# Reordering the start, the first block's close and the last block of a conditioned transformer block

## The chip, the cores and the metric

The kernel runs on one core of a Trainium2 chip. The metric is the device time of one execution in microseconds (us). A core has five engines with queues of their own: TensorE (PE) for matmuls, VectorE (DVE), ScalarE (ACT), GpSimd (POOL), and SyncE (SP), which here issues nearly all DMAs. Each engine works its queue in order; engines wait for each other through semaphores.

## What is computed

One transformer block with adaptive layer norm, for x of shape (8, 1024, 512) in float32, 16 heads of 32 columns, an MLP of 2048:

```python
mod = silu(condition) @ Wada + bada
sh_a, sc_a, gt_a, sh_m, sc_m, gt_m = split(mod, 6, axis=1)
xn = layernorm(x) * g1 + be1
xm = xn * (1 + sc_a) + sh_a
x = x + gt_a * attention(xm)          # causal; qkv = xm @ Wqkv, then @ Wproj + bproj
xn = layernorm(x) * g2 + be2
xm = xn * (1 + sc_m) + sh_m
x = x + gt_m * (gelu(xm @ W1 + b1) @ W2 + b2)
```

## The kernel before

The 8 sequences of 1024 tokens are cut into 16 blocks of 512 tokens, numbered 0 to 15. Even blocks are the first half of a sequence and attend to themselves; odd blocks attend to both halves. The 16 heads go in four groups of four (`g` 0 to 3).

The program is written out by Python in the order in which it is to run: what each engine does is fixed by the order of emission. Two streams are woven together by a planner that keeps its own estimate of each engine's time (`now`, `note`, `due`).

**The attention stream** (`attend`, line 1390). For each group of each block it sends *score tiles* (`scores`, L1206: up to 512 columns for four heads into the PSUM tile `st`; DVE adds the mask at L1218 and takes row maxima at L1226; `maxima_rows` brings the maxima to where they are subtracted, L1266) and *weight units* (`weights_T`, L1292 and L1303 into the same PSUM tile `st`; ACT takes the exponential at L1315; POOL clears the diagonal's upper half at L1320). A first-half block has 3 weight units per group and 3 score tiles, a second-half block 7 and 7. Weight units are the *slots* of the stream. In each slot the unit before is closed: `close` calls `weigh` (L1343, weights times values into `po`), POOL adds the weights up for the denominator (L1427), and after the last unit of a group `finish` sums over partitions by a matmul with ones (L1361), ACT copies (L1367, L1370), DVE inverts in four parts (L1376), and POOL writes the quotient over q (L1381). When group 3 of a block has its quotient, the block is "attended". After closing, a slot sends score tiles ahead for the next group, as far as `upto` says:

```python
                    upto = len(units)
                    if nxt < len(groups):
                        lo, m = first_unit[groups[nxt]], len(score_units(*groups[nxt]))
                        upto = lo + min(m, -(-(k + 2) * m // n_slots))
```

Group 3 of block 0 so has three score tiles of block 1 sent in its first slot, two in its second, and two more in its third, after two that were sent with group 2; and since a unit is closed in the slot after it, the last one of block 0 is closed after block 1's first weight unit.

**The linear stream** (`linear`, `perform`, line 1011) works through a list of steps per window, `plan` (line 228). Steps are: modulation columns (`mod`), gates, transposing and modulating normalized tokens (`at` for attention, `mt` for the MLP, both `modulated`, L622 and L593/L599), projections `k`, `q`, `v` (`strassen`: seven half-size products instead of eight, L199), the output projection with the residual (`proj`, `project_out`, which starts when its block is attended and ends with the second norm), up-projections `u` (four of them) and down-projections `d` (four parts, seven products in all). Some steps run as *side threads* beside the main list (`start`): `at`, `mt`, and the last two products of each `strassen`. `work` (line 1104) sends the next piece of the thread that waits least; at a tie, the side thread's. Attention waits (`step_aside`, L1133) let linear work in, and a pace (`stream`) keeps the two in step. For the values of block 15 attention stops until `v` of that block is done (`close`, line 1440).

The second norm has DVE statistics (L539), then two ACT steps, a root (L547) and the normalizing (L558). While both streams run, these two are *excursions*: `run_excursions(1)` lets one out per slot (line 1415).

**Weights** come through a ring of nine tiles of 256 KB in the order of the steps' pieces (`order`, `fetch`, L328 to L332, on SP); a tile is refilled when it is released. The seven products need sums of quarters of each weight. For the first use of k, q and v these sums are made on the core (`weight_sums`, L668, four DVE subtractions or additions of 128x512) and kept in DRAM (L659, on SP); those of the MLP are prepared along the way on DVE or POOL (`preparation`, `either`, L156 or L159).

**The start** (window -1). `at 0` transposes block 0 into the PSUM tile `early` (of four banks) without the gains, then waits for them:

```python
        if key == "a0":
            written["early"] = 0.0
            yield ["columns"], []
            for c in range(NC):
                modulate(c, early[:, c, :], "st")
```

and the second modulation waits for `early`, so its matmuls stand behind the sixteen transposes. **The end.** Window 15 has the MLP of block 13 to finish (`late`: three down parts), the projection of block 14, `v` of block 15 and most of block 14's MLP; window 16 has the last two down parts of block 14, and block 15's projection and MLP.

Of the kernel before, what the change touches and what calls it, by code (L numbers as in the profile page):

```python
# [22 lines left out]
def kernel(  # L23
# [36 lines left out]
    P = 128  # L60
# [164 lines left out]
    def mlp_steps(n):  # L225
        return [("u", n, i) for i in range(NQ)] + [("d", n, part) for part in range(4)]

    plan = {
        -1: [("at", 0), ("mod", 0), ("mod", 1), ("norm_columns_a",), ("load_xa", 1)]
        + [("k", 0), ("norm_a", 1), ("q", 0), ("at", 1), ("v", 0)],  # L230
        0: [("load_xa", 2), ("preps",), ("k", 1), ("norm_a", 2), ("gates", "a"), ("q", 1)]
# [3 lines left out]
    for w in range(1, NB):  # L235
        n = w - 1
        m = mlp_steps(n)
        even = blocks[n][1] == 0
        rows_a = [("rows", blocks[n][0], "a")] if even else []
        rows_m = [("rows", blocks[n][0], "m")] if even else []  # L240
        own = m[:1] + ([("load_xa", w + 2)] if w + 2 < NB else []) + m[1:3]
        own += [("norm_a", w + 2)] if w + 2 < NB else []
        if w == NB - 1:
            steps = late + [("load_xr", n)] + rows_a + [("proj", n), ("v", w)]
            steps += [("mt", n)] + rows_m + own + m[3:6]
            late = m[6:]
        else:

            steps = late + [("v", w), ("load_xr", n)] + rows_a + [("proj", n), ("k", w + 1)]
            if w == 1:  # L250
                steps = [("load_xr", n)] + rows_a + [("proj", n)]
            steps += [("mt", n), ("q", w + 1)] + rows_m + own
            at = [("at", w + 2)] if w + 2 < NB else []
            if blocks[w][1] == 0:

                steps += m[3:5]
                late = m[5:6] + at + m[6:]
            else:
                steps += m[3:6] + at
                late = m[6:]  # L260
        plan[w] = steps
    n = NB - 1
    plan[NB] = [("load_xr", n), late[0], ("proj", n), late[1], ("mt", n)] + mlp_steps(n)

# [20 lines left out]
    def pieces_of(step):  # L285

        kind = step[0]
        if kind == "mod":
            return [(Wada, step[1], kh, fh) for kh, fh in RAW]
        if kind == "gates":  # L290
            return [(Wada, GATES[step[1]][0], kh, fh) for kh, fh in RAW]
        if kind == "proj":
            return [(Wproj, 0, k) for k in range(NC)]
        if kind == "d":
            return [
                (W2, i, *AT[a]) if a in AT else (W2, i, a)
                for a in DOWN_ORDER[step[2]]
                for i in range(NQ)
            ]
        if raw_step(step):  # L300
            return [(*source_of(step), kh, fh) for kh, fh in RAW]
# [143 lines left out]
    columns_of = {}  # L445
    written["columns"] = written["early"] = NEVER
    gate_rows = {}
# [80 lines left out]
    def normalize(tiles, key, sources):  # L528
# [24 lines left out]
        def apply():  # L553
            for t, xt in enumerate(tiles):
                xh = xt
                if key[0] == "m":
                    xh = tmp.tile([P, D], F32, tag="hat", name=f"xh_{key}_{t}", bufs=NTT)
                nc.scalar.activation(  # L558
                    xh, xt, AF.Identity, bias=offset[:, t : t + 1], scale=rstd[:, t : t + 1]
                )  # L560
                note_act(800, None, [("rstd", key)], [("hat", key, t)])
                got.append(xh)
            hats[key] = got
# [3 lines left out]

    def modulated(key, b, guards):
        for t in ("B11", "B21", "B22", "T1", "T2", "T3", "T4"):
# [17 lines left out]
        at = {t: (key, t) for t in part}  # L587

        def modulate(c, place, source):
            gain, shift = columns_of[key[0]]  # L590
            writes = [at["B11"], at["T1"]] if c < 2 else [at["B21"], at["B22"]]
            if sooner([source], writes, 770, 780) == "DVE":
                nc.vector.tensor_scalar(  # L593
                    xm[:, c, :], place, gain[:, c, b : b + 1], shift[:, c, b : b + 1],
                    ALU.mult, ALU.add,
                )
                note("DVE", 770, [source], writes)
            else:
                nc.scalar.activation(  # L599
                    xm[:, c, :], place, AF.Identity,  # L600
                    bias=shift[:, c, b : b + 1], scale=gain[:, c, b : b + 1],
                )
                note_act(780, None, [source], writes)
# [4 lines left out]
        if key == "a0":  # L608

            early = ps_st.tile([P, NC, TB], F32, tag="st", name="early")  # L610
        for c in range(NC):
            if key != "a0":
                if c:
                    yield [("hat", key, 0)], [BANK]
                bank = lin_bank()
                place, source = banks[bank], ("l", bank)
            else:
                place, source = early[:, c, :], "st"
            for t in range(NTT):
                if t or c:  # L620
                    yield [("hat", key, t)], []
                nc.tensor.transpose(place[:, ts(t, P)], got[t][:, ts(c, P)], ident)  # L622
                note_pe(TR, "whole", [("hat", key, t)], [source])
            if key != "a0":
                modulate(c, place, source)
                live[bank] = False
        if key == "a0":
            written["early"] = 0.0
            yield ["columns"], []
            for c in range(NC):  # L630
                modulate(c, early[:, c, :], "st")
        nc.vector.tensor_tensor(part["T2"], part["B22"], part["T1"], ALU.subtract)  # L632
# [28 lines left out]
    def weight_sums(step, part):  # L661
# [4 lines left out]
        for j, (out, a, b, op) in enumerate(SUMS):  # L666
            got[out] = stage[:, j, :].rearrange("p (k n) -> p k n", n=HB)
            nc.vector.tensor_tensor(got[out], got[a], got[b], op)  # L668
            note("DVE", 700, [], [("sums", *step, out)], port=True)
            keep(w, i, out, stage[:, j, :])  # L670
# [26 lines left out]
    def run_preparation(everything=False):  # L697
        while prepared[0] is not None:
# [4 lines left out]
            try:  # L703
                prepared[0][1] = next(prepared[0][0])
            except StopIteration:
                prepared[0] = None

    tail_key = [None]

    def strassen(step, x, dest, target, row, done):  # L710
# [300 lines left out]
    def perform(step):  # L1011
# [3 lines left out]
        elif kind == "norm_columns_a":  # L1015
            columns_of["a"] = norm_columns("a", 0, 1, O_G1, O_BE1)
            written["columns"] = 0.0
        elif kind == "gates":
# [22 lines left out]
        elif kind == "at":  # L1041
            n = step[1]
            guards = [("m used", n - 3)] if n > 2 else [("v done", 0)] if n == 2 else []
            start(modulated(f"a{n}", blocks[n][0], guards))
        elif kind == "mt":
            n = step[1]
            guards = [("v done", n + 1)]
            start(modulated(f"m{n}", blocks[n][0], guards))
        elif kind == "k":
# [340 lines left out]
    def attend():  # L1390
        previous = None
        for n in range(NB):
# [19 lines left out]
            for g, k, upto in slots:  # L1412
# [9 lines left out]
                if k > 0:  # L1422
                    acc, first = totals[n, g]
                    for _, c0, w in parts:
                        for j in range(HPG):
                            into = acc[:, j, TB - w :]
                            nc.gpsimd.tensor_tensor(into, into, pT[:, j, c0 : c0 + w], ALU.add)  # L1427
# [113 lines left out]
```

## Time and profile before

| | us |
|---|---|
| median of 3 runs | 3687.08 (3687.07 to 3687.18) |
| profiled execution | 3685.5 |
| its span, first to last instruction | 3683.6 |
| PE busy | 3578.0 |
| DVE, POOL, ACT busy | 2158.7, 2030.0, 1330.8 |

The profile is of one execution. Its page gives busy time, the span in 40 slices (busy tenths) and the costliest groups; the trace behind it can be asked for busy time by stage, for waits and for a timeline. A wait is idle time of an engine ahead of an instruction, with the instruction or DMA that ended it. The granted clock of PE is 1.00 when it runs at full speed and 0.5 when at half; over the whole span it was 0.992. [...]

### The profile page before, as it was taken

The page shows a single profiled execution, that of the slowest core. Times are in us where ns is not written, and L with a number is a line of the kernel's source. Part 1 is how long each engine was busy: PE and PEld are TensorE (multiplying, and loading weights), DVE is VectorE, ACT ScalarE, POOL GpSimd, SP SyncE. Part 2 cuts the span into 40 slices and gives each one's busy share as a digit, 9 for nine tenths or more (in the row PEclk, how much of TensorE's full clock was granted, in tenths as well). Part 3 has the DMA queues.
Part 4 walks back from the last instruction along what each step waited for, and adds up shares of the span by engine and source line. Part 5 has one row for each costly group of instructions (what it writes and reads, how often), then busy time and mean ns, then how long its engine had stood idle before and what let it go on. Part 6 is the DMA issues. An engine that isn't in the chain of part 4 may idle for free.

```text
span 3683.6 us, 121126 instructions
## 1 busy us (share of the span) xinstructions
PE 3578.0 (97%) x54821; PEld 1770.6 (48%) x54821; DVE 2158.7 (59%) x2455; ACT 1330.8 (36%) x1415; POOL 2030.0 (55%) x2052
## 2 busy tenths in 40 slices
PE   7979999999999999999999999999999999998989
PEld 4424445445454455544545454454544445454445
DVE  5756676564755647465564656646666465664542
ACT  2324334252343523335242352424524244341421
POOL 1676745656456563556636665356653556445661
PEclk9989999999999999999999999999999999999999
DMA  5642333434334343433434333343333433334334
GB/s 182 202 135 90 109 106 105 127 102 130 102 114 119 108 123 110 131 95 107 125 107 139 96 96 119 111 133 102 102 119 111 136 105 108 107 106 123 90 110 133
DMA packets 307893, 430.34 MB, mean 117 GB/s; under 512 B 25900, under 2 KB 176236, under 8 KB 307380
## 3 DMA queue, kind: packets, MB, share of 16 engines
q1 hardware_dynamic: 307264, 422.56, 38.2%
q8 instruction: 432, 7.08, 0.8%
q14 instruction: 81, 0.66, 0.1%
q10 hardware_dynamic: 116, 0.03, 0.0%
HBM read 394.12 MB, written 28.38 MB: 115 GB/s over the span
## 4 chain that ended last, share of the span: by engine, by line
PE 86%; DVE 7%; ACT 2%; POOL 2%; issue 2%; DMA 0%; SPq 0%; ACTq 0%; POOLq 0%; DVEq 0%
PE bank L199 58%; PE st L1292 8%; PE sc L1206 8%; PE po L1343 7%; DVE mx L1226 2%; PE st L1303 2%; PE bank L1361 2%; POOL pT L1427 1%; PE bank L622 1%; ACT pT L1315 1%; DVE hT L928 1%; DVE sc L1218 1%; DVE xr L156 1%; DVE t_m L156 1%; PE bank L1266 0%
## 5 line engine op out<-in xcount | busy, mean ns | idle before, releaser
L1427 POOL TENSOR_TENSOR pT<-pT,pT 128x512 f32<-128x512 f32 (+3 forms) x1280 | 1209.0, 979 | 550.1 <-ACT pT L1315 383.8
L1315 ACT ACTIVATE pT<-st 128x2048 f32<-128x2048 f32 (+1 forms) x320 | 546.6, 1708 | 1019.4 <-PE st L1303 956.9
L199 PE MATMUL bank<-w,hT 128*32 128x256 f32 x14336 | 808.7, 380 | 5.0 <-DVE hT L928 2.2
L1226 DVE TENSOR_REDUCE mx<-sc 128x4 f32<-128x2048 f32 (+3 forms) x384 | 669.0, 1756 | 208.2 <-PE sc L1206 201.6
L199 PEld LDWEIGHTS bank<-w,hT 128*32 128x32 f32 x14336 | 453.2, 110 | 357.9 <-issue 61.3
L199 PE MATMUL bank<-xm_m,w 128*32 128x256 f32 x8192 | 506.4, 380 | 0.8 <-DVE u_u L191 0.8
L1320 POOL TENSOR_SCALAR_AFFINE_SELECT pT<-pT 128x512 f32<-128x512 f32 x256 | 178.1, 708 | 575.2 <-ACT pT L1315 574.9
L199 PE MATMUL bank<-t_m,w 128*32 128x256 f32 x6144 | 383.1, 380 | 2.4 <-DVE t_m L632 1.0
L1292 PE MATMUL st<-qT,kT 32*128 32x512 f32 (+3 forms) x3072 | 342.9, 530 | 35.9 <-DVE mx L1226 34.7
L199 PEld LDWEIGHTS bank<-xm_m,w 128*32 128x32 f32 x8192 | 254.3, 110 | 249.3 <-issue 95.8
L1206 PE MATMUL sc<-kT,qT 32*128 32x512 f32 (+3 forms) x3072 | 340.2, 527 | 12.6 <-DVE mx L1226 6.5
L1343 PE MATMUL po<-pT,v 128*32 128x512 f32 (+3 forms) x3072 | 315.1, 497 | 6.5 <-POOL pT L1320 6.5
L1218 DVE TENSOR_TENSOR sc<-sc,mask 128x512 f32<-128x512 f32 (+1 forms) x192 | 168.0, 875 | 249.4 <-PE sc L1206 221.6
L199 PEld LDWEIGHTS bank<-t_m,w 128*32 128x32 f32 x6144 | 193.0, 110 | 174.3 <-issue 50.2
L199 PE MATMUL bank<-w,qT 128*32 128x512 f32 x2048 | 241.5, 598 | 6.1 <-POOL qT L1381 3.2
L199 PE MATMUL bank<-xm_a,w 128*32 128x256 f32 x3968 | 244.2, 382 | 2.0 <-ACT xm_a L599 2.0
L1376 DVE RECIPROCAL rec<-rec 128x128 f32<-128x128 f32 x256 | 223.7, 918 | 21.6 <-ACT rec L1367 21.6
L1292 PEld LDWEIGHTS st<-qT,kT 32*128 32x128 f32 x3072 | 129.7, 185 | 201.9 <-issue 60.6
L1206 PEld LDWEIGHTS sc<-kT,qT 32*128 32x128 f32 x3072 | 126.7, 184 | 176.0 <-ACT pT L1315 84.7
L191 DVE TENSOR_TENSOR hT<-bank,u_u 128x512 f32<-128x512 f32 x192 | 130.4, 686 | 120.4 <-PE bank L199 118.4
L199 PE MATMUL bank<-t_a,w 128*32 128x256 f32 x2944 | 186.6, 382 | 0.0
L1315 ACT ACT_TABLE_LOAD x88 | 112.9, 1283 | 183.5 <-PE st L1303 182.8
(184 smaller groups left out, 3546.8 us busy)
## 6 DMA issues: line engine op xcount, KB each, us to landing
w<-in_L_cond_W_dram SPq DMA_DIRECT2D x384, 256.0 KB, 2.9
w<-kept_up_S SPq DMA_DIRECT2D x256, 256.0 KB, 2.6
w<-kept_down_S SPq DMA_DIRECT2D x256, 256.0 KB, 2.7
w<-kept_qkv_S SPq DMA_DIRECT2D x180, 256.0 KB, 2.9
w<-in_L_cond_Wqkv_dram SPq DMA_DIRECT2D x147, 256.0 KB, 3.5
hat<-in_x_dram SPq DMA_DIRECT2D x64, 256.0 KB, 3.4
w<-in_L_cond_Wproj_dram SPq DMA_DIRECT2D x64, 256.0 KB, 3.4
xr<-in_x_dram SPq DMA_DIRECT2D x64, 256.0 KB, 4.4
```

Of the source, the lines that this page charges most:

```text
L156: nc.vector.tensor_tensor(out, a, b, op)
L191: nc.vector.tensor_tensor(out, src, other, op)
L199: nc.tensor.matmul(ps[r, :], lhsT[:, r], rhs, start=start, stop=stop, skip_group_check=True)
L1206: nc.tensor.matmul(sc[:, j, c0 : c0 + w], qTs[n][r, g, ts(qt, P)], keys_of(n, kh)[r, g, :w], start=True, stop=True, skip_group_check=True,)
L1218: nc.vector.tensor_tensor(diagonal, diagonal, mask[:, :span].unsqueeze(1).to_broadcast([P, HPG, span]), ALU.add,)
L1226: nc.vector.tensor_reduce(mx[:, kh, qt, :], sc[:, :, c0 : c0 + w], axis=AX.X, op=ALU.max)
L1292: nc.tensor.matmul(st[:, j, c0 : c0 + w], kT[r, g, ts(k % NTT, P)], qT[r, g, TB - w :], start=(c0 == 0), stop=False, skip_group_check=True,)
L1315: nc.scalar.activation(pT[:, :, :used], st[:, :, :used], AF.Exp, scale=scale)
L1320: nc.gpsimd.affine_select(diagonal, diagonal, pattern=[[0, HPG], [1, P]], compare_op=ALU.is_ge, fill=0.0, base=0, channel_multiplier=-1,)
L1343: nc.tensor.matmul(po[r, TB - w :], v[:, k % NTT, g * P + j * hd : g * P + (j + 1) * hd], pT[:, j, c0 : c0 + w], start=(k == 0), stop=last ...
L1376: nc.vector.reciprocal(some, some)
L1427: nc.gpsimd.tensor_tensor(into, into, pT[:, j, c0 : c0 + w], ALU.add)
```

## The change

Three edits.

1. *Start.* In window -1 the modulations go first, then a new step `sums` for k, q and v each, well ahead of their projections; the sums are made on POOL instead of DVE. `at 0` follows the gains and goes through the three ordinary banks, as every other block's does. A one-column square root loads the ACT table early, and the normalizing of block 0 alternates between ACT and DVE.
2. *Block 0's last group.* Its first and second slots send no score tiles of block 1; in the third, one tile is sent, then the unit just made is closed at once (values, denominator, quotient), then the other six tiles follow.
3. *End.* In window 15 only the first of the three old down parts stays ahead of block 14's projection and `mt`; the other two follow, then `v`. In window 16 the last down part of block 14 runs as a side thread (`beside`) next to block 15's projection instead of behind it.

```diff
-        -1: [("at", 0), ("mod", 0), ("mod", 1), ("norm_columns_a",), ("load_xa", 1)]
-        + [("k", 0), ("norm_a", 1), ("q", 0), ("at", 1), ("v", 0)],
+        -1: [("mod", 0), ("mod", 1), ("sums", "k", 0), ("norm_columns_a",), ("at", 0)]
+        + [("load_xa", 1), ("sums", "q", 0), ("k", 0), ("norm_a", 1), ("q", 0)]
+        + [("sums", "v", 0), ("at", 1), ("v", 0)],
...
         if w == NB - 1:
-            steps = late + [("load_xr", n)] + rows_a + [("proj", n), ("v", w)]
-            steps += [("mt", n)] + rows_m + own + m[3:6]
+            steps = late[:1] + [("load_xr", n)] + rows_a + [("proj", n), ("mt", n)] + late[1:]
+            steps += [("v", w)] + rows_m + own + m[3:6]
...
-    plan[NB] = [("load_xr", n), late[0], ("proj", n), late[1], ("mt", n)] + mlp_steps(n)
+    plan[NB] = [("load_xr", n), late[0], ("beside", late[1]), ("proj", n), ("mt", n)] + mlp_steps(n)
...
+    warm = const.tile([P, 1], F32, tag="warm", name="warm")
+    nc.scalar.activation(warm, eps, AF.Sqrt)
+    table[0] = "sqrt"
...
-        yield ["early"] if i == 1 else [], [BANK]
+        yield [], [BANK]
...
+                if key == "a0" and t % 2:
+                    nc.vector.tensor_scalar(
+                        xh, xt, rstd[:, t : t + 1], offset[:, t : t + 1], ALU.mult, ALU.add
+                    )
+                    note("DVE", 700, [("rstd", key)], [("hat", key, t)])
...
-            nc.vector.tensor_tensor(got[out], got[a], got[b], op)
-            note("DVE", 700, [], [("sums", *step, out)], port=True)
+            nc.gpsimd.tensor_tensor(got[out], got[a], got[b], op)
+            keys = [("sums", *step, x) for x in (a, b)]
+            note("POOL", 1290, keys, [("sums", *step, out)])
...
+    def sum_weights(step):
+        at = take(4)
+        part = {kf: halves(j) for kf, j in zip(RAW, at)}
+        w = weight_sums(step, part)
+        w.update({a: part[kf] for a, kf in AT.items()})
+        summed[step] = at, w
...
-            at = take(4)
-            part = {kf: halves(j) for kf, j in zip(RAW, at)}
-            w = weight_sums(step, part)
+            at, w = summed.pop(step)
...
+        elif kind == "beside":
+            start(perform(step[1]))
+        elif kind == "sums":
+            sum_weights(step[1:])
...
+                        if (n, g) == (0, NC - 1) and k < n_slots - 1:
+                            upto = lo + k
...
+                if (n, g, k) == (0, NC - 1, n_slots - 1):
+
+                    next_scores()
+                    close(*previous)
+                    previous = None
...
+                if previous is None:
+                    maxima_rows()
```

In `modulated`, the part for `early` goes: each column's transposes now take a bank and are modulated at once, for block 0 too, with the gains handed in.

More of the change, by code (lines that the diff above doesn't have):

```diff
@@ L291, in pieces_of @@
             return [(Wada, GATES[step[1]][0], kh, fh) for kh, fh in RAW]
+        if kind == "beside":
+            return pieces_of(step[1])
         if kind == "proj":
@@ L299, in pieces_of @@
             ]
+        if kind == "sums":
+            return [(*source_of(step[1:]), kh, fh) for kh, fh in RAW]
         if raw_step(step):
-            return [(*source_of(step), kh, fh) for kh, fh in RAW]
+            return []
         if kind in ("k", "q", "v", "u"):
@@ L445 @@
     columns_of = {}
-    written["columns"] = written["early"] = NEVER
     gate_rows = {}
@@ L557, in apply @@
                     xh = tmp.tile([P, D], F32, tag="hat", name=f"xh_{key}_{t}", bufs=NTT)
[L558 to L561, printed above, removed]
+                if key == "a0" and t % 2:
[3 more added lines that the diff above has]
+                    note("DVE", 700, [("rstd", key)], [("hat", key, t)])
+                else:
+                    nc.scalar.activation(
+                        xh, xt, AF.Identity, bias=offset[:, t : t + 1], scale=rstd[:, t : t + 1]
+                    )
+                    note_act(800, None, [("rstd", key)], [("hat", key, t)])
                 got.append(xh)
@@ L566, in normalize, with modulated @@
             add_job(lambda t=t: statistics(t), [sources[t]], key[0] == "m")
-    def modulated(key, b, guards):
+    def modulated(key, gain, shift, b, guards):
         for t in ("B11", "B21", "B22", "T1", "T2", "T3", "T4"):
@@ L587, in modulated @@
         at = {t: (key, t) for t in part}
-        def modulate(c, place, source):
-            gain, shift = columns_of[key[0]]
+        for c in range(NC):
+            if c:
+                yield [("hat", key, 0)], [BANK]
+            bank = lin_bank()
+            for t in range(NTT):
+                if t:
+                    yield [("hat", key, t)], []
+                nc.tensor.transpose(banks[bank][:, ts(t, P)], got[t][:, ts(c, P)], ident)
+                note_pe(TR, "whole", [("hat", key, t)], [("l", bank)])
             writes = [at["B11"], at["T1"]] if c < 2 else [at["B21"], at["B22"]]
-            if sooner([source], writes, 770, 780) == "DVE":
+            if sooner([("l", bank)], writes, 770, 780) == "DVE":
                 nc.vector.tensor_scalar(
-                    xm[:, c, :], place, gain[:, c, b : b + 1], shift[:, c, b : b + 1],
+                    xm[:, c, :], banks[bank], gain[:, c, b : b + 1], shift[:, c, b : b + 1],
                     ALU.mult, ALU.add,
                 )
-                note("DVE", 770, [source], writes)
+                note("DVE", 770, [("l", bank)], writes)
             else:
                 nc.scalar.activation(
-                    xm[:, c, :], place, AF.Identity,
+                    xm[:, c, :], banks[bank], AF.Identity,
                     bias=shift[:, c, b : b + 1], scale=gain[:, c, b : b + 1],
                 )
-                note_act(780, None, [source], writes)
+                note_act(780, None, [("l", bank)], writes)
+            live[bank] = False
             if c == 1:
@@ L606, in modulate @@
                 note("DVE", 700, [at["B11"], at["T1"]], [at["T1"]], port=True)
[L608 to L631, printed above, removed]
         nc.vector.tensor_tensor(part["T2"], part["B22"], part["T1"], ALU.subtract)
@@ L706, in run_preparation @@
                 prepared[0] = None
+    summed = {}
+    def sum_weights(step):
[4 more added lines that the diff above has]
+        summed[step] = at, w
     tail_key = [None]
@@ L1016, in perform @@
             columns_of["a"] = norm_columns("a", 0, 1, O_G1, O_BE1)
-            written["columns"] = 0.0
         elif kind == "gates":
@@ L1043, in perform @@
             guards = [("m used", n - 3)] if n > 2 else [("v done", 0)] if n == 2 else []
-            start(modulated(f"a{n}", blocks[n][0], guards))
+            start(modulated(f"a{n}", *columns_of["a"], blocks[n][0], guards))
+        elif kind == "beside":
+            start(perform(step[1]))
+        elif kind == "sums":
+            sum_weights(step[1:])
         elif kind == "mt":
@@ L1047, in perform @@
             guards = [("v done", n + 1)]
-            start(modulated(f"m{n}", blocks[n][0], guards))
+            start(modulated(f"m{n}", *columns_of["m"], blocks[n][0], guards))
         elif kind == "k":
```

## The prediction

> **What bounds the kernel now.** I read the page first, for the engines' shares.
>
> ```profile
> PE 3578.0 (97%) x54821; PEld 1770.6 (48%) x54821; DVE 2158.7 (59%) x2455; ACT 1330.8 (36%) x1415; POOL 2030.0 (55%) x2052
> ...
> PE   7979999999999999999999999999999999998989
> ```
>
> PE is the bound; only slices 0, 2 and two near the end fall short. So a microsecond is won only where PE stands still or runs at half clock. The second view is the table of busy time by stage, with stage borders put at PE's gaps (columns: stretch, its length, busy PE, PEld, DVE, ACT, POOL, then the granted clock).
>
> ```profile
> 22.70:34.00 11.30, 8.67 (x88) 3.72 (x92) 6.33 (x8) 2.50 (x4) 1.76 (x1) 0.55 0.70 239
> ...
> 54.00:70.00 16.00, 12.66 (x168) 7.98 (x166) 13.89 (x15) 3.40 (x5) 1.77 (x1) 0.89 0.44 149
> 70.00:175.00 105.00, 102.89 (x1784) 52.57 (x1776) 78.20 (x93) 35.43 (x39) 56.83 (x70) 1.00 0.59 189
> 175.00:221.00 46.00, 28.35 (x217) 9.10 (x220) 24.75 (x27) 10.20 (x8) 29.02 (x33) 0.70 0.54 182
> 221.00:262.00 41.00, 41.00 (x529) 16.53 (x522) 29.97 (x34) 10.25 (x8) 39.41 (x38) 1.00 0.47 150
> 262.00:283.00 21.00, 13.02 (x76) 3.38 (x75) 10.62 (x10) 10.57 (x12) 8.57 (x8) 0.84 0.08 23
> 283.00:3300.00 3017.00, 2986.83 (x45788) 1477.75 (x45790) 1813.16 (x2045) 1144.30 (x1213) 1699.46 (x1723) 1.00 0.38 112
> ...
> 3339.00:3368.00 29.00, 26.17 (x360) 11.40 (x356) 11.51 (x19) 1.18 (x2) 16.44 (x16) 1.00 0.66 206
> 3368.00:3393.00 25.00, 17.92 (x156) 6.59 (x148) 11.36 (x13) 13.04 (x15) 5.49 (x10) 0.86 0.12 34
> ```
>
> Five holes stand out: the start, 175 to 221, 262 to 283, 3339 to 3393 and the end. The 3017 us between hold only 30 us of idle. The timeline says what each hole waits for (start, duration, engine, line, idle before it).
>
> ```profile
> 22.66 3.26 PE L199 MATMUL bank<-xm_a,w 128*32 128x256 f32 x32 [1.98 <-ACT xm_a L599]
> ...
> 25.98 1.75 DVE L668 TENSOR_TENSOR sums_k<-w,w 128x512 f32<-128x512 f32 x1
> ...
> 28.52 3.64 PE L199 MATMUL bank<-t_a,sums_k 128*32 128x256 f32 x32 [2.60 <-DVE sums_k L668]
> ...
> 63.24 2.42 PE L199 MATMUL bank<-sums_v,t_a 128*32 128x256 f32 x32 [2.57 <-DVE sums_v L668]
> ```
>
> ```profile
> 179.59 5.94 POOL L1427 TENSOR_TENSOR pT<-pT,pT 128x384 f32<-128x384 f32 x8
> ...
> 189.04 1.23 PE L1292 MATMUL st<-qT,kT 32*128 32x256 f32 x8 [4.58 <-DVE mx L1226]
> ...
> 202.62 2.09 PE L1292 MATMUL st<-qT,kT 32*128 32x512 f32 x8 [2.41 <-DVE mx L1226]
> ...
> 216.49 1.27 POOL L1381 TENSOR_TENSOR qT<-top,rec 128x512 f32<-128x512 f32 x1 [0.30 <-DVE rec L1376]
> ```
>
> ```profile
> 3352.46 3.64 PE L199 MATMUL bank<-w,qT 128*32 128x512 f32 x32 [2.83 <-DVE y L191]
> ...
> 3550.16 12.73 PE L199 MATMUL bank<-w,qT 128*32 128x512 f32 x104 [3.25 <-POOL qT L1381]
> ```
>
> From 180 to 220 there is no linear matmul: the next one is block 0's output projection, which needs the quotient at 216.49. PE runs scores only, each waiting for DVE's maximum.
>
> **The start (sums on GpSimd, modulation first, square-root table early, half the normalizing on DVE).** Now k's first product starts at 22.66 because the second modulation runs behind the sixteen transposes, and its gains are ready at 21.7. After the change both modulations come first. Their last weights are the twelfth transfer of 256 KB; at the stage's 239 GB/s twelve take 13.2 us, so about 15 us in, and the second modulation ends near 15.7 (estimate). Sixteen transposes at the cold 3.04/13 = 0.23 us end near 19.4; three banks suffice, since a modulate (0.78 us) frees one in less than four transposes take. Normalizing is done by then with or without the table load (1.28 us) moved, so those two edits are worth nothing by themselves: transposes wait for the modulations. k's first product starts at 19.4, 3.3 us earlier. Its second needs S2 and T2. S2 is the second of four sums on POOL, 1.27 us each as in POOL's 128x512 rows, after k's pieces at about 18.5: 21.1. T2 follows the last modulate (20.5) by one subtraction. Here a rule speaks against the change: the Trainium skill's page "SBUF — State Buffer", section "Who interferes with whom", says that a DVE instruction with two SBUF inputs and a GpSimd one exclude each other for a whole instruction. The row agrees: the first k sum on DVE took 1.75 us beside a POOL subtraction and 0.69 us alone. T1 and T2 are two such instructions, now against eight POOL sums in a row: without contention T2 is there at 21.2 and PE doesn't wait; by the rule at 20.5 + 1.75 plus what is left of T1's 1.06, up to 23.3. The first product (3.26 cold) ends at 22.7; I take 22.9. Against 28.52 that is 5.6 us. From 28.5 to 33.8 PE ran at half clock, a loss of 2.6; denser work should save half: 1.3. Bounds: 3 to 8.5.
>
> Sums of v wait 2.57 us at 63.24, followed by 3.4 us at half clock (0.89 over the 16 us), 1.7 lost: together 4.3. Afterwards POOL, idle from 30 to 60, has them long before; T2 of block 1 is ready at 60.0, and 0.77 us of waiting for scores stays. Start: 5.6 + 1.3 + 4.3 = **11 us** (7 to 14). The twelve stores of sums on SP now wait for POOL ahead of block 1's x tiles: these issue at about 23.5 instead of 23.0 and are read at 42.6, hidden by 15 us. If that cover went, PE would wait at block 1's transposes, at most 3 us. Stages up to 175 are PE-bound (2.1 us idle in 105), so the gain arrives at the first hole whole.
>
> **First block closed early.** In times of before: group 3 of block 0 sends its three weight units at 159.2, 175.0 and 189.0, with seven score tiles of block 1 between and two more behind. The change sends the three in succession. POOL then sets the end: diagonals 0.64 + 1.23, accumulation 5.94, group 2's quotient 1.28, diagonal 0.64, accumulation 2.77, in sum 12.5, plus 2.9 waiting for the second exponential, from 162.6: 178. Ones-matmul 1.04, copy 0.59, four reciprocals 3.6 with one maximum (2.29) among them, quotient 1.27: 187 instead of 217.8. PE until 187: linear work left at 159 is 5.5 products of 1.73 and sixteen gate matmuls of 0.23, 13.2 us; weights 3.7, values 3.4, ones 2.1, three score tiles 3.4: 25.8 of 28 us. The added wait is that of the last values and the ones-matmul: on PE score tiles and linear work sent later are queued behind them, and DVE's maxima wait in turn. While linear work lasts it is sent ahead; when it is gone, about 180, two score tiles (2.3 us) fill the last 7: 5 idle, and I add 1 for the in-order wait behind POOL. Below: 2. Above: POOL also has weight preparations (5.3 us for four), then 12.
>
> Clock: the page "TensorE: Matmul & The Clock Gate", "Part 1", lets the array fall to half after one idle window of about 3.4 us and return after one busy one. By that, of these gaps only 4.58 counts, some 3 us lost. The row shows more: 0.70 over 46 us is 27.6 us at half clock, kept down by gaps of 2.41; 512-column tiles took 2.09 instead of 1.14, in sum over the stage 7.5 us. I go by the row: now 17.65 idle + 7.5 = 25.1; afterwards 6 + 2 = 8. **17 us** (by the rule 13; bounds 8 to 23).
>
> The next hole, 262 to 283 (8.0 idle, 2.1 of clock), waits for block 0's second norm: its two ACT steps run one per weight slot, after the projection. With projection and slots both starting about as far apart as now, it stays: **0** (from 10 won to 10 lost; preparations not finished by the first up-projection are pushed out at once then, on POOL, DVE and SP).
>
> **Last block.** The projection of block 14 goes ahead of two MLP parts. Its x tiles and gate rows now queue on SP behind two output stores that wait for POOL until 3342.8, and the row lands at 3351.6; moved ahead of those stores, it issues 3.3 us after the projection begins and lands 4.6 later: 7.9, before the fourth bank is wanted (3 x 3.64 = 10.9). **2.8 us**. Behind the stores come v's pieces instead, held up to 4.8 us; nine pieces of 1.73 us in the ring cover it. One y buffer is held by the unfinished MLP part, so 0.69 + 1.27 + two hand-overs, about 2.5 us per bank, go in series under 3.64 of PE; if POOL is late by over 1.1, it shows. The hole 3368 to 3393 stays: the second norm's ACT steps wait for two weight slots after v, and v ends no earlier. Bounds 0 to 5; 10 more if they ran.
>
> **End.** The last MLP part of block 14 (14 us) runs beside the close instead of behind the projection: it fills 2.3 + 0.5 + 3.25 and saves 1.7 of clock. But it was what hid the last norm: last product to first product of u is 16.0 us now; bare it is y 0.7, add 1.3, statistics 1.2, root 0.8, first hat to u 4.6, about 8.6, with 2.5 of clock. 7.7 won, up to 8 lost: **0** (-3 to +3).
>
> **Sum.** 11 + 17 + 0 + 2.8 + 0 = 31 us off the profiled execution's 3685.5 (span 3683.6, 1.9 around it): 3654.5. The median, 3687.1, is 1.6 above: 3656.
>
> **Rivals and chances.** Forecast, 3648 to 3664: 0.52. *The hole moves* (0.20): the preparations land on POOL between accumulations (12 idle), or the second norm comes as late as now by the clock, not by the projection, and the hole 262 to 283 grows by 8: 31 - 6 - 8 = 17, 3670. For it: POOL is 39.4 of 41 us busy in 221 to 262. *Both close* (0.15): the norm's ACT steps find slots while q still runs: 31 + 10 = 41, 3646; that slots take 8.5 us and q over 18 speaks for it. *Little remains* (0.06): linear work goes first, closing is as late as now, gain of the start partly lost: 3682. *Slower* (0.07): linear work, no longer behind its schedule after block 0, runs out ahead of the quotients at later block ends; 14 blocks with one such wait of 3.6 are 50 us, less 31: 3706. It decides from 2.2 us a block. Against it: the middle's gaps repeat every 445 us whatever the start was.
>
> Faster by over 0.2% (about what a measurement here can tell from no change) 0.87, within 0.06, slower 0.07. Range: 3641 takes in most of the second hole, 3673 the moved one.
>
> **What would show it.** k's second product near 23 and v's sums without a wait; the quotient of group 3 near 176 (187 less 11); 175 to 221 with clock over 0.9; the projection of block 14 without the 2.83; the end with a bare norm of some 8 us. Wrong if the middle's idle exceeds 30 by ten, or the quotient comes after 195.

## The result

The changed kernel takes 3682.28 us (median of 22 runs, 3679.93 to 3684.23). The kernel before, run beside it on the same chip, takes 3687.13 (22 runs, 3682.46 to 3692.41). The ratio is 0.9986, 95% interval 0.9980 to 0.9992: a gain, but 26 us less than forecast and outside the range. The profiled execution of the changed kernel has a span of 3680.8 us and a granted clock of 0.990, where the one before had 3683.6 and 0.992.

The page of the changed kernel, engine shares and PE's 40 slices:

```profile
PE 3573.3 (97%) x54821; PEld 1771.8 (48%) x54821; DVE 2153.9 (59%) x2452; ACT 1327.5 (36%) x1410; POOL 2041.4 (55%) x2062
...
PE   8879999999999999999999999999999999999989
```

Slice 0 went from 7 to 8, and of the two eights near the end one is gone. But slice 2 is still at 7, and slice 1 went from 9 to 8. The table of busy time by stage shows it in numbers (stretch, length, busy PE, PEld, DVE, ACT, POOL, granted clock, DMA share, GB/s):

```profile
22.70:46.00 23.30, 22.68 (x384) 13.42 (x388) 13.60 (x22) 7.01 (x11) 13.37 (x10) 0.93 0.76 251
46.00:62.00 16.00, 16.00 (x260) 9.48 (x256) 12.15 (x14) 3.40 (x5) 1.78 (x1) 1.00 0.58 183
...
167.00:207.00 40.00, 22.00 (x143) 7.53 (x136) 23.69 (x24) 5.35 (x5) 11.98 (x14) 0.64 0.52 180
207.00:253.00 46.00, 44.88 (x544) 16.68 (x536) 31.14 (x37) 11.75 (x11) 38.96 (x35) 0.98 0.40 122
253.00:283.00 30.00, 14.18 (x120) 5.51 (x124) 15.21 (x15) 10.73 (x12) 8.97 (x10) 0.77 0.32 104
283.00:3300.00 3017.00, 2988.60 (x45776) 1477.17 (x45768) 1811.14 (x2045) 1143.01 (x1208) 1704.78 (x1730) 1.00 0.38 112
...
3339.00:3366.00 27.00, 27.00 (x492) 15.67 (x483) 5.24 (x8) 1.17 (x2) 15.77 (x16) 1.00 0.65 192
```

The start is dense, and PE is full from 3339 to 3366, where the 2.83 us wait was. The first hole is still there: 18.0 us idle in 167 to 207 at clock 0.64 (before: 17.65 idle in 175 to 221 at 0.70). The second is twice as large: 15.8 us idle in 253 to 283 at 0.77 (before: 8.0 in 262 to 283 at 0.84). The middle kept its pace, 28.4 us idle where 30.2 were.

### The profile page after: what moved, and what is told of

It reads as the page before. It is cut to its first block, busy times and chain, and to the rows that moved or that the text cites. A ratio compares the mean times of both kernels' runs of the same rounds, so it can differ in the third digit from the quotient of the medians.

```text
span 3680.8 us, 121124 instructions
## 1 busy us (share of the span) xinstructions
PE 3573.3 (97%) x54821; PEld 1771.8 (48%) x54821; DVE 2153.9 (59%) x2452; ACT 1327.5 (36%) x1410; POOL 2041.4 (55%) x2062
## 4 chain that ended last, share of the span: by engine, by line
PE 86%; DVE 7%; POOL 2%; ACT 2%; issue 2%; DMA 0%; SPq 0%; ACTq 0%; POOLq 0%; DVEq 0%
PE bank L199 58%; PE st L1298 8%; PE sc L1212 8%; PE po L1349 7%; DVE mx L1232 2%; POOL pT L1435 2%; PE st L1309 2%; PE bank L1367 1%; PE bank L608 1%; DVE hT L931 1%; DVE sc L1224 1%; ACT pT L1321 1%; DVE xr L156 1%; DVE t_m L156 1%; PE bank L1272 0%
```

## Milestones

A quotient (the POOL line that writes over q) ends the work of one group of one block, so its start is a milestone of the attention stream. The table gives the start of block 0's first quotient, and the others as times after it, so that the start's gain stays in the first column. Each row is one profiled execution; the kernels are those of the experiments below.

| kernel | block 0, group 0 | block 0, group 3 | block 1, group 0 | block 1, group 3 | block 15, group 3, after the one before |
|---|---|---|---|---|---|
| before | 135.2 | +81.3 | +149.7 | +318.1 | +3095.3 |
| the change | 127.2 | +74.2 | +167.8 | +328.6 | +3089.3 |
| `start_alone` | 128.9 | +80.8 | +151.2 | +319.5 | +3095.9 |
| `close_alone` | 134.9 | +74.2 | +167.9 | +328.4 | +3093.5 |
| `end_alone` | 133.6 | +80.0 | +148.5 | +316.8 | +3091.8 |
| `start_end` | 125.2 | +81.0 | +149.5 | +317.8 | +3091.4 |
| `recip_first` | 126.6 | +48.5 | +161.5 | +331.6 | +3083.2 |
| `prep_sooner` | 126.2 | +74.2 | +163.0 | +323.8 | +3090.2 |
| `recip_prep` | 126.9 | +48.5 | +161.7 | +331.2 | +3086.2 |
| `close_now` | 128.6 | +68.6 | +147.9 | +316.4 | +3085.5 |
| `now_prep` | 126.1 | +68.9 | +159.6 | +320.4 | +3091.9 |
| `no_hold` | 127.2 | +71.0 | +149.7 | +314.3 | +3084.9 |

The change brought the fourth quotient 7 us closer, where 31 had been forecast (its end at 187 instead of 217.8), and then the next one came 18 us later than before. The rows with the changed start differ in the first column by up to 3.7 us (125.2 to 128.9), so a few microseconds between two single rows say little.

**Why the quotient came so late.** The timeline of the changed kernel around it:

```profile
172.04 0.59 ACT L1376 COPY top<-po 128x512 f32<-128x512 f32 x1
...
179.71 2.09 PE L1212 MATMUL sc<-kT,qT 32*128 32x384 f32 x16 [3.83 <-DVE mx L1232]
...
195.68 2.29 DVE L1232 TENSOR_REDUCE mx<-sc 128x4 f32<-128x2048 f32 x1 [2.21 <-PE sc L1212]
197.88 3.38 DVE L1382 RECIPROCAL rec<-rec 128x128 f32<-128x128 f32 x4
201.43 1.26 POOL L1387 TENSOR_TENSOR qT<-top,rec 128x512 f32<-128x512 f32 x1 [5.85 <-DVE rec L1382]
```

Values and denominator were copied out by about 172, yet DVE inverts at 197.9. The inversions are jobs that the planner sends when it thinks that DVE has time; it sent them behind the maxima of the six score tiles of block 1 that follow the close, and DVE works in order. On PE the linear work had ended at 172.9, so these score tiles ran alone, and from the second on each waited for a maximum (1.89, 3.83, 3.82, 2.16 and 2.40 us).

**Why the second hole grew.** The same kernel, where the second norm of block 0 should pass:

```profile
249.13 0.30 ACT L554 ACTIVATE rstd_m<-mv_m,eps 128x4 f32<-128x4 f32 x1
...
254.03 2.00 SPq L681 DMA_DIRECT2D prep_down<-in_L_cond_W_dram  x4
...
259.87 2.15 DVE L156 TENSOR_TENSOR prep_down<-prep_down 128x512 f32<-128x512 f32 x3 [10.58 <-DMA prep_down<-in_L_cond_W_dram]
...
266.23 2.09 PE L1298 MATMUL st<-qT,kT 32*128 32x512 f32 x8 [13.23 <-DVE mx L1232]
...
271.93 2.92 ACT L571 ACTIVATE xh_m<-xr,offset_m,rstd_m 128x512 f32<-128x512 f32 x4
```

One weight preparation was left when the first up-projection was to be sent. The code then pushes out all that is left (line 885): a load, sums on DVE and POOL, stores. The sums stand in DVE's queue ahead of everything and wait 10.58 us for the load. Behind them wait a maximum, for which PE stands 13.23 us, and the 0.17 us reciprocal of the second norm's root (261.93, 12.5 us after the root). The normalizing follows the root by 22.8 us; in the kernel before it was 7.9:

```profile
271.79 0.30 ACT L547 ACTIVATE rstd_m<-mv_m,eps 128x4 f32<-128x4 f32 x1
...
279.64 2.92 ACT L558 ACTIVATE xh_m<-xr,offset_m,rstd_m 128x512 f32<-128x512 f32 x4
```

## Experiments

Each kernel was timed in turns with the kernel before; the medians of before lay at 3686.5 to 3687.1. Differences between two experiments are taken from their medians; set against each one's own runs of before they change by 0.6 us at most. None leaves out or changes any of the computation.

**One part alone (`start_alone`, `close_alone`, `end_alone`).** The first is the changed kernel with edits 2 and 3 undone, the others the kernel before with only edit 2 or 3:

```diff
+                        if (n, g) == (0, NC - 1) and k < n_slots - 1:
+                            upto = lo + k
...
+                if (n, g, k) == (0, NC - 1, n_slots - 1):
+                    next_scores()
+                    close(*previous)
+                    previous = None
...
+                if previous is None:
+                    maxima_rows()
```

(edit 2, all that `close_alone` has over the kernel before.)

> The changed start alone, with the first block's close and the end as in the kernel before. The two traces put side by side give the changed kernel some 9.6 us of advantage on TensorE after 70 us. If the close is what lost it again (theory: reciprocals queued behind maxima, then preparations forced out on the queue of DVE), the start alone keeps it: 3677.5 us (3675 to 3680), quotient of block 0's group 3 near 208, hole before block 0's second norm about 8 us as before. Rival: the holes swallow the start's gain whatever the close does, because DVE and the preparations set their ends: 3683 to 3687.

> The early close of block 0 alone, start and end as in the kernel before. Theory: nothing is won in the first hole, since the four reciprocals are sent behind the maxima of six score tiles, and the second hole grows by some 7 us because preparations are forced out: 3691 us (3688 to 3696). Rival, the prediction's own account of this part: 17 us won, 3670.

> The new order of the last two windows alone. From the traces: 2.8 us less waiting of the projection of block 14 for its gate row, and nothing on balance at the very end, where 6 us of waiting for the quotient become 6 us of a bare second norm: 3684 us (3682 to 3686). Rival: the bare norm and the half clock after it cost more than the wait did: 3687 or above.

Measured: start 3680.78 (ratio 0.9983, 0.9974 to 0.9992), close 3692.24 (1.0017, 1.0008 to 1.0026), end 3682.82 (0.9989, 0.9980 to 0.9998). That is -5.8, +5.7 and -3.8 us; their sum, -3.9, is the whole change's -4.9 within the intervals. So the parts add up, and the one from which most was expected is the one that costs. `close_alone` and `end_alone` fell into their expected ranges; `start_alone` is 0.8 us above its own, with the quotient at 209.6 (expected near 208) and 7.3 us idle in 253 to 283, so its second hole did not grow. `close_alone` repeats the changed kernel's milestones to 0.2 us (+74.2, +167.9, +328.4), with 16.3 us idle in 253 to 283: the early close does the same whatever the start was, and the growth of the second hole belongs to it.

**The change without its early close (`start_end`).**

```diff
-                        if (n, g) == (0, NC - 1) and k < n_slots - 1:
-                            upto = lo + k
...
-                if (n, g, k) == (0, NC - 1, n_slots - 1):
-                    next_scores()
-                    close(*previous)
-                    previous = None
...
-                if previous is None:
-                    maxima_rows()
```

> The changed start and the changed end without the early close. The parts measured alone gave 5.8 and 3.8 us; if they add up, 3677 us (3674 to 3680), 5 us below the whole change. Rival: the parts overlap, and it is no better than the whole change: 3681 or more.

Measured: 3675.08 (0.9970, 0.9959 to 0.9981). It is within the expected range, and 7.2 us faster than the changed kernel, which gives the early close's cost a second time.

**The inversions at once (`recip_first`).**

```diff
                     close(*previous)
                     previous = None
+                    run_jobs(True)
```

> The changed kernel, with the pending DVE jobs (four reciprocals and the quotient of block 0's group 3) sent at once after the early close, ahead of the other six score tiles. Theory: these reciprocals, sent behind six tiles' maxima, are what kept the quotient at 201 us. Then the quotient comes at 176 to 183, the projection starts by 185, idle time of TensorE from 167 to 207 falls from 18 to below 8, and the whole is 3674 us (3669 to 3679); part may be lost again to the forced preparations in the second hole. Rival: GpSimd's accumulation and preparations hold the quotient; it then stays past 195 and the time at 3681 to 3684.

Measured: 3681.01 (0.9985, 0.9976 to 0.9993). The mechanism held: the fourth quotient comes at 175.1. The time missed the expectation: it didn't move. The timeline and the table by stage of this kernel show why:

```profile
175.12 1.26 POOL L1387 TENSOR_TENSOR qT<-top,rec 128x512 f32<-128x512 f32 x1 [5.25 <-DVE rec L1382]
```

```profile
167.00:207.00 40.00, 33.94 (x339) 11.56 (x341) 29.82 (x37) 4.71 (x6) 20.20 (x20) 0.96 0.56 173
207.00:253.00 46.00, 32.31 (x352) 13.68 (x348) 21.92 (x23) 15.33 (x14) 27.81 (x23) 0.81 0.62 201
...
400.00:455.00 55.00, 40.35 (x432) 15.70 (x428) 21.99 (x24) 18.95 (x15) 36.70 (x39) 0.81 0.12 38
```

```profile
225.93 2.87 DVE L156 TENSOR_TENSOR prep_down<-prep_down 128x512 f32<-128x512 f32 x4 [11.33 <-DMA prep_down<-in_L_cond_W_dram]
...
231.34 2.09 PE L1298 MATMUL st<-qT,kT 32*128 32x512 f32 x8 [11.07 <-DVE mx L1232]
```

The first hole is gone (6.1 us idle at clock 0.96), but the linear stream now arrives at the up-projections sooner still, so the preparations are forced again (11.33 us), and its work is used up by 400: to 455 PE runs 40.35 of 55 us, where the changed kernel ran 51.82, and block 1's last quotient comes no sooner. This is the forecast's rival *slower*, linear work running out ahead of the quotient, at one place only.

**Preparations sooner (`prep_sooner`, `recip_prep`).** A preparation is let out 6 instead of 12 us after its load was sent, by the planner's own time, in the changed kernel and in `recip_first`.

```diff
-                ready = now["PE"] + 12000
+                ready = now["PE"] + 6000
```

> The changed kernel with the weight preparations allowed 6 us after their loads are sent instead of 12, so that the last ones are not forced out, loads and all, when the first up-projection is sent. Theory: the 13.2 us gap of TensorE at 266 is DVE waiting for the load of a forced preparation. Then this gap falls below 5 us and the lag gained in 253 to 283 falls from 18 to 8 or less. If time won there stays won: 3674 us (3670 to 3677). Rival, holes move on: linear work is then out earlier at the end of block 1, a hole opens between 400 and 440, and the whole stays at 3680 to 3683.

> Both the reciprocals sent at once and the preparations at 6 us. If the two holes are causes of their own, 18 us of the first and 10 of the second are won: 3660 to 3668. If attention, held back by the early close and bound by DVE, sets when block 1 ends, the last quotient of block 1 stays near 455 and the time comes back as idle between 380 and 450: 3674 to 3681.

Measured: 3670.06 (0.9956, 0.9945 to 0.9968) and 3681.03 (0.9984, 0.9975 to 0.9992). In `prep_sooner` the last preparation is through before the up-projections: nothing waits 10 us on DVE (4.53 at most), 253 to 283 has 5.7 us idle instead of 15.8, no hole opens at 400 to 455 (3.2 us idle in both), and the median is 12.2 us lower, at the lower edge of what was expected. Its profiled execution is the slowest of its six (3668.73 to 3677.8), and in it block 15's last quotient comes only 4.9 us sooner. With both edits the time is that of `recip_first`, 11 us above `prep_sooner`: the preparations still came too late for the quicker linear stream (a wait of 11.85 us), and block 1's last quotient stands at +331.2 (458.1 us, expected near 455). So the two holes are not separate causes that can be added; the second reading of the expectation, that attention sets block 1's end, held.

**Close first, invert at once, nothing held back (`close_now`).**

```diff
-                        if (n, g) == (0, NC - 1) and k < n_slots - 1:
-                            upto = lo + k
...
-                    next_scores()
                     close(*previous)
                     previous = None
+                    run_jobs(True)
```

> The changed start and end; block 0's last unit is closed at once and its reciprocals sent ahead, but the first two slots of group 3 send their score tiles of block 1 as before, so attention isn't put behind. If what the changed kernel lost was attention's lead (score tiles held back), the quotient comes near 190, no hole opens at 400 to 440, and the gain over start and end alone is 5 to 10 us: 3669 us (3666 to 3673). Rival: any earlier quotient only brings the first up-projection, and with it the forced preparations, forward: the hole of 253 to 283 grows by as much, 3677.

Measured: 3667.47 (0.9946, 0.9934 to 0.9958), near the expected number, though the quotient comes at 197.2 and not near 190. Three edits differ from the changed kernel, so the next one takes them apart.

**Only the hold-back taken out (`no_hold`).**

```diff
-                        if (n, g) == (0, NC - 1) and k < n_slots - 1:
-                            upto = lo + k
```

> The changed kernel with its hold-back taken out: group 3 of block 0 again sends three and two score tiles of block 1 in its first two slots; the third slot still sends one tile, closes, then sends what is left. Theory A: the hold-back is what costs. With it all seven score tiles, and with them seven maxima of 2.29 us on VectorE, stand behind the last weight unit, where no linear work is left, and the reciprocals queue behind them. Without it only two or three are left: quotient of group 3 near 199 us, the holes up to 283 us lose 12 to 15 us less than in the changed kernel, median 3668 to 3671, about the 3667.5 of the kernel that closes first and inverts at once. Theory B: sending the reciprocals at once is what made that kernel fast; then this one stays at 3678 to 3683 with the quotient at or after 201.

Measured: 3662.75 (0.9937, 0.9925 to 0.9949), the fastest of all, 24 us under the kernel before, 19.5 under the changed one, and 5 under the expected range. Its table by stage:

```profile
167.00:207.00 40.00, 26.60 (x204) 8.76 (x207) 22.11 (x26) 8.31 (x7) 26.16 (x31) 0.74 0.63 209
207.00:253.00 46.00, 44.30 (x547) 17.01 (x540) 35.57 (x42) 13.74 (x12) 38.99 (x37) 1.00 0.45 143
253.00:283.00 30.00, 28.82 (x363) 12.71 (x364) 21.44 (x19) 13.15 (x14) 16.06 (x12) 1.00 0.29 92
```

The quotient comes 3 us sooner than in the changed kernel (198.2), the first hole has 13.4 us idle instead of 18.0, and the second has all but closed (1.2 us idle, clock 1.00). The last preparation's sums run at 237.2 on DVE and at 245.3 on POOL, with no wait for a load, and the normalizing follows the root by 9.0 us. Theory A held in direction; inverting at once, theory B, is not what made `close_now` fast. Why `close_now` is 4.7 us slower than this kernel was not followed.

Set beside `start_end`, which has no edit 2 at all, `no_hold` also says what the early close is worth by itself: 3662.75 against 3675.08, 12.3 us won. That lies within the 8 to 23 of the forecast, but by luck, for it is not won where the forecast put it: in these two profiles the first hole has 3.3 us less idle (13.4 for 16.7) and the second, for which the forecast was 0, 7.0 less (1.2 for 8.2). Edit 2 is thus two things: closing at once wins 12.3, and holding score tiles back costs 19.5. It is the hold-back that makes the quotient early: without it the last weight unit of block 0 is sent at 181.0, with it at 158.3. So the fastest kernel has its quotient 23 us later than `recip_first`.

**The last edits tried on `close_now` and on the changed kernel (`now_prep`, `gains_pool`, `now_gains`).** The first is the 6000 of `prep_sooner` in `close_now`; the others move the first norm's four gain columns to GpSimd, in the changed kernel and in `close_now`:

```diff
-        -1: [("mod", 0), ("mod", 1), ("sums", "k", 0), ("norm_columns_a",), ("at", 0)]
+        -1: [("mod", 0), ("mod", 1), ("norm_columns_a",), ("sums", "k", 0), ("at", 0)]
...
+        on = nc.gpsimd if name == "a" else nc.vector
-        nc.vector.tensor_scalar(one_plus, modT[:, ts(gain_at, NC), :], 1.0, None, ALU.add)
+        on.tensor_scalar(one_plus, modT[:, ts(gain_at, NC), :], 1.0, None, ALU.add)
...
```

(The other three column operations move in the same way.)

> The best kernel so far (no hold-back, close at once, reciprocals at once: 3667.5) with the preparations let out 6 instead of 12 us after their load. Theory A: the 12 us that sooner preparations were worth in the changed kernel came from the forced last preparation at 253 to 263 us; in this one the last preparation is kept at 243.7, before the first up-projection, so nothing is forced and nothing is won: 3665 to 3670. Rival: VectorE and GpSimd spread their load better wherever preparations are sooner; then 3655 to 3660.

> The changed kernel with the four gain columns of the first norm (128x32 each) made on GpSimd, ahead of the sums of k, instead of on VectorE beside them. Theory A: in the changed kernel these four took 3.4 us (19.05 to 22.40) because two of them wait out a sum on GpSimd, against 0.73 us alone; on one engine in a row they don't collide: k's first product starts 1.5 to 2.5 us earlier, near 22, quotient (0,0) near 125.5, median 3679 to 3681. Rival: GpSimd's own small instructions are as slow as the wait, or the sums of k come later by as much and the second product waits: start of the second product not before 26.8, no gain, 3682.

> The same edit of the gain columns on the best kernel so far (3667.5). Theory A: a gain at the start goes through to the end where nothing is forced later: 3664.5 to 3666.5. Rival: the hole at block 0's end takes it back, 3667 to 3669.

Measured: 3677.32 (0.9974, 0.9965 to 0.9983), 3682.76 (0.9991, 0.9982 to 1.0000) and 3667.81 (0.9950, 0.9937 to 0.9962). `now_prep` was a miss on both sides: 10 us slower than without. The timelines of the second norm, in `close_now` and then in `now_prep`:

```profile
234.25 0.66 DVE L546 BATCH_NORM_STATS2 st_m<-xr 128x6 f32<-128x512 f32 x1
...
252.85 2.92 ACT L571 ACTIVATE xh_m<-xr,offset_m,rstd_m 128x512 f32<-128x512 f32 x4
```

```profile
243.37 0.66 DVE L546 BATCH_NORM_STATS2 st_m<-xr 128x6 f32<-128x512 f32 x1
...
262.67 2.92 ACT L571 ACTIVATE xh_m<-xr,offset_m,rstd_m 128x512 f32<-128x512 f32 x4
```

The last of the four statistics comes 9.1 us later. The last residual addition of y ran on DVE in `close_now` (225.37); in `now_prep` it runs on POOL behind an accumulation of 5.43 us (226.82), two more additions of a bias row follow it, and the last ends at 229.9 instead of 226.1. The statistics, and the two ACT steps behind them, then go out later by about a slot. So sooner preparations don't help where none is forced, and what they displace can cost as much. Why the planner shifted just this addition was not followed further.

`gains_pool` removed the collision that it was made for: the four columns take 1.14 us in a row on POOL, where they had taken 3.35 beside the sums, and k's products start sooner.

```profile
21.66 2.48 PE L199 MATMUL bank<-xm_a,w 128*32 128x256 f32 x32
...
24.58 1.93 PE L199 MATMUL bank<-t_a,sums_k 128*32 128x256 f32 x32 [0.43 <-DVE t_a L628]
...
32.35 2.15 PE L199 MATMUL bank<-t_a,sums_k 128*32 128x256 f32 x24 [2.39 <-POOL t_a L159]
```

These are 2.25 and 2.27 us sooner than in the changed kernel, but a later product now waits 2.39 us for a sum of token quarters that stands on POOL behind the sums of q, and a product that started at 35.98 in the changed kernel starts at 37.52. Block 0's first quotient comes at 128.6 (expected near 125.5; 127.2 in the changed kernel). The times are those of the rivals, in both kernels, but not by their route: the sums of k did not make the second product wait, and in `now_gains` too the first quotient (128.0 against 128.6 in `close_now`) comes within the spread of the rows above, long before the hole at block 0's end.

## Why the prediction was wrong, step by step

- **The early close, forecast 17 us won (8 to 23): 5.7 lost by itself, 7.2 within the change.** Two steps failed. The first is the sum "four reciprocals 3.6 with one maximum (2.29) among them, quotient 1.27: 187". The chain up to the denominator was right: forecast 179 in times of before (178 and 1.04), measured 171.3, after a start that is 8 us sooner. But "with one maximum among them" supposed that the planner sends the inversions at once. They were sent behind the maxima of six score tiles, and the quotient came at 201.4; the prediction had named a quotient after 195 as a sign of being wrong. `recip_first`, which sends the inversions at once, ends the quotient at 176.4, the 176 of the forecast.
- **The second step that failed, and the one that cost the time, is the term that put the held-back score tiles at nothing.** The forecast counted PE's work (25.8 of 28 us) and took it that score tiles fill the gap; behind DVE they come 3.4 to 5.9 us apart (starts at 174.74, 179.71, 185.63, 189.03, 193.52). What the hold-back does to DVE was not costed. In 150 to 172, with linear work to cover them, DVE spends 9.2 us on maxima before, 3.2 in the changed kernel and 7.7 in `no_hold`; the rest runs after 173, when linear work is gone (stretch, length, busy DVE on maxima, clock, DMA share, GB/s; in this order):

```profile
150.00:172.00 22.00, 9.17 (x4) 1.00 0.65 204
```

```profile
150.00:172.00 22.00, 3.15 (x2) 1.00 0.54 167
```

```profile
150.00:172.00 22.00, 7.73 (x4) 1.00 0.75 246
```

  `no_hold` against the changed kernel prices this term at 19.5 us, and while it stands an early quotient wins nothing (175 in `recip_first`). Of the idle time that `no_hold` saves, 4.6 us lie in the first hole and 14.6 in the second, where the load of the last preparation is sent at 213.69 and not, forced, at 254.03. So most of the cost arrives through the preparations. That the held-back maxima are why the planner sent them late is argued, not shown: no run separates the two.
- **The second hole, forecast 0 (10 won to 10 lost): about 8 lost.** Idle went from 8.0 to 15.8, within the bounds; it is part of what the early close cost, not a loss beside it. The text named the cause, preparations "pushed out at once", as a bound only. It is the rival *the hole moves* in kind, in place and in size, though that rival still had the first hole give 11. *Little remains* named the number, 3682, but by another route: the closing was not late, the inversions were, so that agreement is chance.
- **The start, forecast 11 (7 to 14): 7.6.** Block 0's first quotient starts at 127.0 in the mean of the nine profiles with this edit alone in the start, 134.6 in the three without; in time, `start_alone` wins 5.8. Sums of v no longer make PE wait. The term that was mis-sized is k's second product, 5.6 us: it started at 26.85 where 22.9 was forecast and 28.52 measured before, 1.7 us won. The first started at 23.91 instead of 19.4:

```profile
18.04 0.72 PE L199 MATMUL bank<-condT,w 128*32 128x8 f32 x40 [2.98 <-issue]
...
23.91 3.18 PE L199 MATMUL bank<-xm_a,w 128*32 128x256 f32 x32
...
26.85 2.41 PE L199 MATMUL bank<-t_a,sums_k 128*32 128x256 f32 x32
```

  Two things made it late. The second modulation's last matmuls waited 2.98 us at 18.04 for something that the trace doesn't name, so it ended at 18.8 and not at 15.7. And the gain columns collided with the sums (3.35 us, against 0.73 in the kernel before):

```profile
19.81 1.32 POOL L663 TENSOR_TENSOR sums_k<-sums_k,w 128x512 f32<-128x512 f32 x1
19.91 1.27 DVE L449 TENSOR_TENSOR shifta<-onepa,cols 128x32 f32<-128x32 f32 x1
21.09 1.25 POOL L663 TENSOR_TENSOR sums_k<-w,w 128x512 f32<-128x512 f32 x1
21.21 1.19 DVE L450 TENSOR_TENSOR shifta<-shifta,modT 128x32 f32<-128x32 f32 x1
```

  The rule of the Trainium skill's page "SBUF — State Buffer", section "Who interferes with whom", was put to T1 and T2 only. It bites more on the smallest instructions: one of 0.18 us took 1.27, a whole sum's length. The trace of the kernel before had shown it: there the same operation for the second norm took 1.30 us at 185.50, beside a quotient of 1.26 us on POOL at 185.49.
- **The last block, forecast 2.8 (0 to 5): right.** The wait of 2.83 is gone, and from block 14's last quotient to block 15's there are 276.6 us instead of 278.2, in `end_alone` 275.0; the other rows with the new end lie at 274.3 to 278.0 and those without it at 277.8 and 281.1, so the size is known only roughly. **The end, forecast 0 (-3 to +3): right.** From block 15's last quotient to the first product of u it is 30.5 us, 30.1 before; the bare norm shows as 6.05 us of idle and half clock, 11.1 us from the last product to the first of u, which is the 8.6 and 2.5 worked out. `end_alone` gives the two together 3.8 us.
- **The clock** was right to be read from the rows. In the changed kernel it falls in the gap before 179.71 (granted 1.00 until 176, 0.50 from 179.7 on) and stays at half past 205: 28.8 us of the 40 from 167 to 207. A score tile of 512 columns takes 1.14 us at 174.74 and 2.09 at 193.52. By the Trainium skill's page "TensorE: Matmul & The Clock Gate", "Part 1", full speed returns after a busy window of about 3.4 us, and until 202.57 no group of matmuls here ran 2.7 us without a gap. The prediction's 13 "by the rule" counted the gaps and left that out. Nor does the fall need a gap of the page's 3.4 us: in the kernel before it came after one of 2.41.

```profile
211.24 1.14 PE L1206 MATMUL sc<-kT,qT 32*128 32x512 f32 x8 [1.05 <-ACT pT L1315]
...
214.79 2.09 PE L1292 MATMUL st<-qT,kT 32*128 32x512 f32 x8 [2.41 <-DVE mx L1226]
```

What stays open: why `prep_sooner` wins 12 us in the median and under 5 in its profiled execution, what the second modulation waits for, and by which path the hold-back makes the last preparation late.

## What to carry to other kernels

When a tail is pulled forward by holding other work back, ask what that work ran beside: here score tiles that wait for DVE lost their linear cover, and holding them back cost 19.5 us where the earlier tail won 12.3. An early result is worth something only if what it releases isn't used up before the next slow stage; follow one milestone per stage to the end of the next block before counting it. Where a queue is written in advance by estimates, cost an edit by the order that it really produces on the engine next on the chain, and look for code that flushes leftovers at a deadline.

## What was not expected of the hardware

- A DVE instruction on 128x32 with two SBUF inputs took 1.19 and 1.27 us beside GpSimd sums of 1.25 to 1.32 us, and 0.18 to 0.19 without (0.24 and 0.25 when done by GpSimd itself, in `gains_pool`).
- In the changed kernel the array stayed at half clock for 28.8 of 40 us, with gaps of 1.87 to 3.83 us between groups of matmuls of 1.2 to 2.6 us; in the kernel before it fell to half after a gap of 2.41 us.
